# Batches half the layers apart, slab-wise keys and values, and maxima on a clock of slab lengths, in a four-layer cross-attention kernel

## The chip, the core and the metric

The kernel runs on one core of one Trainium2 chip. A core has five engines that run side by side and each take their instructions strictly in order: TensorE (PE, matmuls; its weight loads are listed apart as PEld), VectorE (DVE), ScalarE (ACT), GpSimd (POOL) and SyncE (SP), which here only issues DMA transfers. The metric is the device time of one execution in microseconds (us). The clock granted to PE varies during a run; the profile gives it as a share of full speed (PEclk).

## The reference, cut to what matters

`x` is 16 batches of 256 tokens with 128 channels, `ctx` is 16 batches of 1601 keys with 64 channels. Four layers follow each other; each is a cross-attention to `ctx` and a feed-forward part, all with residuals:

```python
x = x + L0_xattn(ln(x), ctx)   # 16 heads of 8: causal self-attention plus attention to ctx
x = x + L0_ffn(ln(x))          # 32 experts, top 4
x = x + L1_xattn(ln(x), ctx)   # 16 heads of 8
x = x + L1_ffn(ln(x))          # quantised linear, depthwise convolution, silu, quantised linear
x = x + L2_xattn(ln(x), ctx)   # 16 heads of 32: self-attention block, then attention to ctx, each with a gelu part
x = x + L2_ffn(ln(x))          # 8 experts, top 1
x = x + L3_xattn(ln(x), ctx)   # 16 heads of 8
x = x + L3_ffn(ln(x))          # 16 experts, top 2, plus a shared one
```

Every attention to `ctx` is `softmax(q k^T * scale) v` over 1601 keys in float32. Batches don't depend on each other; inside one batch everything is a chain.

## The kernel before, in words

**Slabs.** An attention to `ctx` of one batch and layer is done in 4 slabs of 4 heads (`attend`). A slab has two passes. In the first, PE forms the scores of each head `g` with the queries on the partitions (28 units of matmuls, into PSUM banks), and DVE reduces each to a maximum (`mx<-bank`). At the slab's end a short piece of work (rank `ENDS`) turns the maxima into a bfloat16 triple that sums to the negated maximum (`nm`, `nmp`, `thirds`, `shift_T`, ending in the copy `nmT` on ACT). In the second pass there are 7 steps of up to 2 key tiles each: PE forms the scores again with the keys on the partitions and adds `nmT` (`st_ops`), ACT takes the exponential (`exps`, tile `p`), PE multiplies with the values (`weigh`). `normalised` divides. Layers l0, l1, l3 have heads of 8 ("8-slabs"; their sums come with the values), l2 has heads of 32 ("32-slabs"; plain float32 keys). One batch has 12 8-slabs and 4 32-slabs; the program has 256 slabs.

**Keys, queries and their transfers.** For heads of 8, keys and queries are split into a high and a low half (`split`: tiles `hl`, the high half by ACT, the low one by DVE), and each half is spread over the partitions by DMAs issued by SP (`spread`). A set of queries (`queries8`, `parts8`) takes 16 such DMAs of 32 KB. Layer l0 makes three sets for a batch: queries for `ctx`, queries and keys for its own causal attention. The halves of queries live in 3 places (`chan_r`); a place is free when its DMAs have landed.

**Places.** Tiles get places from small classes: 7 PSUM banks, 7 places `k` (keys, their halves, and the raw context `cn`), 2 places `v`, 2 transposed contexts, 6 places `w4` (query and hidden tiles), 4 `mx`. Classes `k`, `v` and the contexts are given out in the order in which the tiles were recorded.

**Who sets the order.** Nothing is issued while the program is recorded: each operation, or a run of them, becomes a unit with a rank `(level, place)`. `emit` then plays the program against costs of its own and writes, for each engine, at each moment, the ready unit of lowest rank that finds its places; for PE it adds up to three more units on other row groups. The levels are CHAIN (layer norms, projections, feed-forward parts, self-attention of l2, keys, values; always first), ENDS, OWN (the causal attention of l0), and STEPS (maxima and steps of the slabs, last). So the slabs fill what the chains leave. The order is fixed when the program is built; on the chip the engines only wait for each other's semaphores. `emit` charges 0.07 us for a DMA issue on SP (`t = 0.07` in `emit`).

**Batches.** The main loop at the end takes batches in pairs (`LANES = 2`). Both batches of a pair are loaded together, and then for each layer the first batch's 4 slabs are followed by the second's. The chain between two layers of one batch runs beside the 4 slabs of the other. The next pair begins after l3 of this one: its loading may start earlier, when places are free.

**Ranks of slabs.** Slabs are counted with `n`. Step `j` of slab `n` has the place `n + j/7`; maximum `i` of 28 has `n - 1 + i/28 - 0.4`. All slabs count as equally long.

Of the kernel before, what the change touches and what calls it, by code (L numbers as in the profile page):

```python
# [17 lines left out]
ALU = mybir.AluOpType  # L18
# [30 lines left out]

CHAIN, ENDS, OWN, STEPS = 0, 1, 2, 3  # L50

LEAD = 0.4
NAHEAD = 2


# [396 lines left out]
def model(ctx: ExitStack, tc: tile.TileContext, d, out):  # L452
# [86 lines left out]
    def bank():  # L539
        return pb.tile([P, 512], F32, tag="bank", name=name("bank"))  # L540
# [5 lines left out]
    def mm(o, l, r, start=True, stop=True, free=False):  # L546
        nc.tensor.matmul(out=o, lhsT=l, rhs=r, start=start, stop=stop, skip_group_check=free)
# [94 lines left out]
    def new(tag, shape, base, dtype=F32, loose=False):  # L642
        return prog.tile(classes[tag], shape and list(shape), dtype, name(base), loose)
# [222 lines left out]
    def exps(att, sc, n, r):  # L866
        e = new("p", [P, 2, T], "p")
        nc.scalar.activation(e[:r, :n, :], sc[:r, :n, :], AF.Exp, scale=att.scale)
        return e

    def values8(tag, nt, z=None):


        v = new(tag, [P, nt * 144 + 24], tag)
        v9 = v[:, :-24].rearrange("p (t h e) -> p t h e", h=H, e=9)
        with prog.behind(z):
            if nt == NT:
# [113 lines left out]
    def value_tiles(x, w):  # L991

        for t0, ms in ((0, (4, 4)), (4, (3, 2))):
            ps2 = [bank(), bank()]
            with prog.together():
                for i in range(ms[0]):
                    for h in range(2):
                        if i < ms[h]:
                            r = rows_of(h * NL + t0 + i)
                            mm(ps2[h][:r, i * P : (i + 1) * P],  # L1000
                               x[h * CC : (h + 1) * CC, (t0 + i) * P : (t0 + i) * P + r], w[h * CC : (h + 1) * CC, :])
            for h in range(2):
# [7 lines left out]
    def keys(ctxT, l):  # L1010
        ks = {}
        if l == "l2":
            for s in range(4):
                t = new("k", [P, NK], "k32")
                for k0, k1, p in halves(wkv2[:, s * P : (s + 1) * P], ctxT[1], NK):
                    evac(t[:, k0:k1], p)
                ks[s] = t
        else:
            hl = [new("k", [P, NKE], "hl", F32R) for _ in range(2)]
            bias = W.get(l + "_bck")  # L1020
            for k0, k1, p in halves(W[l + "_Wck"], ctxT[0], NKE):
                split([t[:, k0:k1] for t in hl], p, bias)
            for s in range(4):
                t = new("k", [P, NKE], "k8", F32R, loose=True)
                spread(t, hl, s, True)
                ks[s] = t
        return ks

    def values(ctxT, l):
        vs = {}  # L1030
        if l == "l2":
            for s in range(4):
                v = new("v", [P, NT, P], "v32")
                for t, m, r, p in value_tiles(ctxT[1], wkv2[:, 512 + s * P : 512 + (s + 1) * P]):
                    evac(v[:r, t : t + m, :].rearrange("p t e -> p (t e)"), p)
                vs[s] = v
        else:
            v, v9 = values8("v", NT, ctxT[0])
            for t, m, r, p in value_tiles(ctxT[0], W[l + "_Wcv"]):
                evac(v9[:r, t : t + m, :, :8], p.rearrange("p (t h e) -> p t h e", t=m, h=H))  # L1040
            vs[0] = v
        return vs

    slab_no = [0]

    def attend(att):

        steps = [(t, min(2, NT - t), rows_of(t)) for t in range(0, NT, 2)]
        w = NKE if att.d8 else NK
        for s in range(4):  # L1050
            mx = new("mx", [P, 2, 4, 4], "mx", loose=True)
            stretches = [(range(q, q + 1), c * 512, c * 512 + 512) for q in range(2) for c in range(3)]
            stretches.append((range(2), 3 * 512, w))
            n = slab_no[0]
            slab_no[0] += 1
            for i, (qs, k0, k1) in enumerate(stretches):
                for g in range(4):
                    with prog.at(STEPS, n - 1 + (4 * i + g) / (4 * len(stretches)) - LEAD):
                        h = slice(32 * g, 32 * g + 32)
                        m, j = k1 - k0, k0 // 512  # L1060
                        p = bank()[:, : m * len(qs)].rearrange("p (q k) -> p q k", k=m)
                        with prog.together((g,)):
                            for q in qs:
                                mm(p[:, q - qs[0], :], att.q[h, s, q * P : (q + 1) * P], att.k[s][h, k0:k1])
                        nc.vector.tensor_reduce(mx[:, qs[0] : qs[-1] + 1, g, j], p, AX.X, ALU.max)
            with prog.at(ENDS):
                nm = new("nm", [P, 2, 4], "nm")
                nc.vector.tensor_reduce(nm, mx, AX.X, ALU.max, negate=True)
                sh = new("nmp", None, "nmp")
                thirds(sh, nm)  # L1070
                nmT = shift_T([sh])[:, 0, :]
            av = None
            for j, (t0, m, r) in enumerate(steps):
                with prog.at(STEPS, n + j / len(steps)):
                    pr = [exps(att, t, m, r) for t in st_ops(att, s, t0, m, r, nmT)]
                    if av is None:
                        av = accumulators("acc")
                    weigh(att, s, av, pr, t0, m, r, t0 + m == NT)
            with prog.at(ENDS):
                normalised(att, s, av)  # L1080
        return att.o


    def route(logits, n, k, gate):
# [277 lines left out]


    prog.recording = True
    for b0 in range(0, nb, LANES):
        lanes = range(b0, min(nb, b0 + LANES))
        ctxTs, lives = {}, {}
        for b in lanes:
            with prog.at(CHAIN):
                ctxTs[b] = load_ctx(b)  # L1370
                lives[b] = life(b, ctxTs[b])
        atts = {}
        for l in LAYERS:
            for b in lanes:
                with prog.at(CHAIN):
                    if l == "l0":
                        atts[b] = next(lives[b])
                with prog.at(CHAIN):
                    ks = keys(ctxTs[b], l)
                    vs = values(ctxTs[b], l)  # L1380
                atts[b].k, atts[b].v = ks, vs
                attend(atts[b])
                with prog.at(CHAIN):
                    atts[b] = next(lives[b], None)
    with tc.manual_schedule():
        prog.emit()

# [118 lines left out]
```

## Time and profile before

| | |
|---|---|
| median of 3 runs | 9560.31 us (9547.48 to 9571.74) |
| the profiled execution's own time | 9500.53 us |
| its span, first to last instruction | 9498.8 us |
| mean granted PE clock | 0.904 |
| PE busy | 8874.5 us (93%) |
| DVE, ACT, POOL busy | 5863.8 us (62%), 5171.3 us (54%), 1080.9 us (11%) |
| DMA issues of queries, `q<-hl` | 1024 of 32 KB, 1.9 us to landing |

How to read it: a busy PE is not a PE at full speed, because a matmul takes about twice as long while the granted clock is 0.5. So the text that follows multiplies the busy share of a stage by its granted clock and calls that the stage's useful share. The program has 8 pairs, and the same pattern comes back about every 1180 us; the second pair (from about 1140 us) is the one shown.

### The profile page before, as it was taken

The numbers are of one execution on the slowest core, as the hardware profiler recorded it, in microseconds if no ns is written. First come the engines' busy times: TensorE is split into PE (matmuls) and PEld (weight loads), VectorE is DVE, ScalarE is ACT, GpSimd is POOL, SyncE is SP. The second block draws the span as 40 slices with busy tenths as digits, with TensorE's granted clock in tenths as the row PEclk, the third lists the DMA queues.
The fourth block names the chain that finished last, engine by engine and source line by source line (L and its number), as shares of the span: only waits on it lengthen the run. The fifth ranks groups of instructions, "written<-read, shape, count | busy, mean of one in ns | idle before, by whom it ended". The sixth has DMA issues, their size and how long they took to land.

```text
span 9498.8 us, 210842 instructions
## 1 busy us (share of the span) xinstructions
PE 8874.5 (93%) x86118; PEld 5239.1 (55%) x86118; DVE 5863.8 (62%) x12308; ACT 5171.3 (54%) x10590; POOL 1080.9 (11%) x2747
## 2 busy tenths in 40 slices
PE   6999899998999989999899998999989999899999
PEld 3556555565555655556455564555645556455565
DVE  4755657556675565755667555676566755567555
ACT  2654556555564555645556454664555645566455
POOL 2011110111101011010110101101010010100100
PEclk7989889898898988989899897898988989899898
DMA  2200212002120021200212002120011101111011
GB/s 55 49 18 15 45 37 54 14 14 48 38 52 11 14 49 36 53 11 18 47 39 49 11 18 46 39 49 11 20 45 44 43 11 21 45 45 44 11 22 32
DMA packets 158879, 313.48 MB, mean 33 GB/s; under 512 B 65163, under 2 KB 116275, under 8 KB 157910
## 3 DMA queue, kind: packets, MB, share of 16 engines
q1 hardware_dynamic: 154676, 297.83, 13.6%
q8 instruction: 678, 11.11, 0.5%
q14 instruction: 291, 2.38, 0.1%
q0 software_dynamic: 768, 1.48, 0.0%
q10 hardware_dynamic: 2466, 0.68, 0.0%
HBM read 98.31 MB, written 2.10 MB: 11 GB/s over the span
## 4 chain that ended last, share of the span: by engine, by line
PE 80%; DVE 8%; ACT 4%; SPq 3%; issue 2%; DMA 2%; POOL 1%; ACTq 0%; DVEq 0%; POOLq 0%
PE bank L395 53%; PE st L395 22%; PE mx L395 4%; DVE mx L395 4%; SPq L395 3%; ACT p L395 3%; DMA k<-hl 1%; DVE z L395 1%; DVE x L395 1%; DVE st L395 1%; DMA ws<-in_s_l3f_dram 1%; DVE mv L395 0%; POOL nmp L395 0%; ACT ctxT L395 0%; DVE rc L395 0%
## 5 line engine op out<-in xcount | busy, mean ns | idle before, releaser
L395 DVE TENSOR_REDUCE mx<-bank 128x1 f32<-128x512 f32 (+2 forms) x7168 | 4093.1, 627 | 1967.6 <-PE bank L395 1871.6
L395 ACT ACTIVATE p<-st 128x512 f32<-128x512 f32 (+1 forms) x7680 | 3849.8, 575 | 2460.8 <-PE st L395 2310.6
L395 PE MATMUL st<-q,k 32*128 32x256 f32 (+1 forms) x18176 | 2531.6, 370 | 154.6 <-ACT p L395 105.7
L395 PE MATMUL bank<-k,q 32*128 32x512 f32 (+2 forms) x10240 | 2375.5, 521 | 174.8 <-DVE hl L395 88.6
L395 PEld LDWEIGHTS st<-q,k 32*128 32x128 f32 (+1 forms) x18176 | 1644.3, 190 | 1011.0 <-issue 361.7
L395 PE MATMUL bank<-p,v 128*32 128x256 f32 (+1 forms) x27648 | 2105.8, 412 | 0.0
L395 PE MATMUL st<-nmT,ones 32*128 32x512 bf16 (+1 forms) x7680 | 1682.0, 389 | 0.0
L395 PEld LDWEIGHTS bank<-k,q 32*128 32x128 f32 x10240 | 1042.2, 198 | 740.5 <-ACT p L395 199.5
L395 PEld LDWEIGHTS bank<-p,v 128*32 128x32 f32 (+1 forms) x27648 | 757.6, 114 | 896.6 <-issue 607.5
L395 POOL CAST nmp<-nm 128x8 bf16<-128x8 f32 x384 | 84.4, 220 | 4852.8 <-DVE nm L395 4465.1
L395 PE MATMUL bank<-p,ones 128*32 128x256 f32 (+1 forms) x7680 | 586.2, 384 | 0.0
L395 PEld LDWEIGHTS <-ones 32*128 32x128 bf16 (+1 forms) x7680 | 485.8, 98 | 116.5
L395 DVE TENSOR_REDUCE nm<-mx 128x2 f32<-128x512 f32 (+1 forms) x768 | 378.8, 520 | 253.8 <-PE mx L395 238.0
L395 DVE RECIPROCAL rc<-bank 128x8 f32<-128x8 f32 (+1 forms) x384 | 276.1, 719 | 293.0 <-PE bank L395 287.2
L395 POOL TENSOR_SCALAR_AFFINE_SELECT p<-p 128x512 f32<-128x512 f32 x512 | 300.3, 624 | 701.2 <-PE bank L395 490.0
L395 ACT ACT_TABLE_LOAD x222 | 284.8, 1283 | 149.5 <-PE st L395 108.0
L395 PE MATMUL mx<-k,q 32*128 32x256 f32 x1536 | 305.4, 426 | 63.0 <-DMA k<-hl 42.8
L395 POOL TENSOR_TENSOR rs<-rs,neghalf 128x2 f32<-128x2 f32 x240 | 170.3, 710 | 1663.3 <-DVE rs L395 1648.9
L395 PEld LDWEIGHTS bank<-p,ones 128*32 128x32 f32 (+1 forms) x7680 | 248.5, 111 | 178.0 <-issue 10.6
L395 ACT COPY v<-bank 128x512 f32<-128x512 f32 (+3 forms) x592 | 232.5, 451 | 144.5 <-PE bank L395 143.9
L395 PEld LDWEIGHTS mx<-k,q 32*128 32x128 f32 x1536 | 216.4, 215 | 164.5 <-issue 46.2
L395 PEld LDWEIGHTS bank<-ws,h 128*128 128x128 f32 x1664 | 231.7, 222 | 46.6 <-issue 32.3
(221 smaller groups left out, 6545.0 us busy)
## 6 DMA issues: line engine op xcount, KB each, us to landing
k<-hl SPq DMA_DIRECT2D x768, 200.2 KB, 3.6
q<-hl SPq DMA_DIRECT2D x1024, 32.0 KB, 1.9
ws<-in_s_l_a_li_dram SPq DMA_DIRECT2D x32, 768.0 KB
ws<-in_s_l3f_dram SPq DMA_DIRECT2D x32, 768.0 KB, 7.3
ws<-in_s_l0f_dram SPq DMA_DIRECT2D x32, 512.0 KB, 6.0
ws<-in_s_l_a_qkv_dram SPq DMA_DIRECT2D x16, 768.0 KB, 4.2
k<-hl SPq DMA_DIRECT2D x256, 32.0 KB, 1.9
ws<-in_s_l3f_dram SPq DMA_DIRECT2D x16, 384.0 KB
```

Of the source, the lines that this page charges most:

```text
L395: getattr(getattr(self.nc, e), method)(*a, **k)
```

## The change

- **The order of batches.** `slabs_in_order` writes one list of slabs for the whole program. After a start (l0 of batches 0 and 1, l1 of batch 0) it repeats, for each batch b: l0 of b+1, l2 of b, l1 of b+1, l3 of b (l0 of b+1 is left out for b = 0, where it has gone already). Between two layers of one batch there are always 4 or 8 slabs of another, except where the program starts and ends: l2 of batch 0 directly follows l1 of batch 0, and l3 of batch 15 directly follows l2 of batch 15. A batch is loaded alone (`begun`), recorded just before the first slab of l3 of the batch two before it.
- **Keys and values of l2** are recorded slab by slab (`keys32`, `val32`), each before its slab, and no longer four of each ahead of the layer.
- **The steps wait for the values:** each step's units, the scores and exponentials too, now depend on the writers of the values (`prog.behind`).
- **Ranks.** `clock` gives each slab a beginning on a time line in planner microseconds, 18 for an 8-slab and 34 for a 32-slab. Its steps are spread over that length. Its 28 maxima are spread over 18 us that end at least 4 us before the beginning.

```diff
-LEAD = 0.4
+LONG8, LONG32, LONGM, LEAD = 18, 34, 18, 4
...
+    def attend(att, s, begin, ahead):
...
-                    with prog.at(STEPS, n - 1 + (4 * i + g) / (4 * len(stretches)) - LEAD):
+                with prog.at(STEPS, ahead + (4 * i + g) * LONGM / (4 * len(chunks))):
...
-                with prog.at(STEPS, n + j / len(steps)):
+            with prog.at(STEPS, begin + j * (LONG8 if att.d8 else LONG32) / len(steps)), prog.behind(att.v[0 if att.d8 else s]):
...
+    def slabs_in_order():
+        def whole(b, l):
+            return [(b, l, s) for s in range(4)] if b < nb else []
+
+        seq = whole(0, "l0") + whole(1, "l0") + whole(0, "l1")
+        for b in range(nb):
+            x, y = whole(b, "l2"), whole(b + 1, "l0") if b else []
+            if y:
+                seq += y + x
+            else:
+                seq += x
+            seq += whole(b + 1, "l1") + whole(b, "l3")
+        return seq
+
+    def clock(seq):
+        begin, t = [], 0.0
+        for _, l, _ in seq:
+            begin.append(t)
+            t += LONG32 if l == "l2" else LONG8
+        ahead, t = [], 1e9
+        for t0 in reversed(begin):
+            t = min(t, t0 - LEAD) - LONGM
+            ahead.append(t)
+        return list(zip(seq, begin, reversed(ahead)))
...
-    for b0 in range(0, nb, LANES):
...
-        for l in LAYERS:
-            for b in lanes:
...
-                    ks = keys(ctxTs[b], l)
-                    vs = values(ctxTs[b], l)
-                atts[b].k, atts[b].v = ks, vs
-                attend(atts[b])
+    begun(0)
+    begun(1)
+    for (b, l, s), begin, ahead in clock(slabs_in_order()):
+        att, ctxT = atts[b], ctxTs[b]
+        with prog.at(CHAIN):
+            if l == "l2":
+                att.k[s], att.v[s] = keys32(ctxT, s), val32(ctxT, s)
+            elif s == 0:
+                att.k, att.v[0] = keys8(ctxT, l), val8(ctxT, l)
+        if l == "l3" and s == 0:
+            begun(b + 2)
+        attend(att, s, begin, ahead)
+        if s == 3:
+            with prog.at(CHAIN):
+                atts[b] = next(lives[b], None)
```

`begun(b)` loads the context and `x` of batch b and records its life up to the queries of l0. `keys8` and `val8` are the old branches for heads of 8.

More of the change, by code (lines that the diff above doesn't have):

```diff
@@ L1008, in value_tiles, with keys8 @@
                     yield t + whole, 1, r, ps2[h][:r, whole * P : m * P]
-    def keys(ctxT, l):
+    def keys8(ctxT, l):
         ks = {}
[L1012 to L1026, printed above, removed]
-        return ks
@@ L1029, in values @@
[L1029 to L1042, printed above, removed]
@@ L1044, in model, with keys32 @@
-    slab_no = [0]
-    def attend(att):
+        hl = [new("k", [P, NKE], "hl", F32R) for _ in range(2)]
+        bias = W.get(l + "_bck")
+        for k0, k1, p in halves(W[l + "_Wck"], ctxT[0], NKE):
+            split([t[:, k0:k1] for t in hl], p, bias)
+        for s in range(4):
+            t = new("k", [P, NKE], "k8", F32R, loose=True)
+            spread(t, hl, s, True)
+            ks[s] = t
+        return ks
+    def keys32(ctxT, s):
+        t = new("k", [P, NK], "k32")
+        for k0, k1, p in halves(wkv2[:, s * P : (s + 1) * P], ctxT[1], NK):
+            evac(t[:, k0:k1], p)
+        return t
@@ new lines, in val8, with val32 @@
+    def val8(ctxT, l):
+        v, v9 = values8("v", NT, ctxT[0])
+        for t, m, r, p in value_tiles(ctxT[0], W[l + "_Wcv"]):
+            evac(v9[:r, t : t + m, :, :8], p.rearrange("p (t h e) -> p t h e", t=m, h=H))
+        return v
+    def val32(ctxT, s):
+        v = new("v", [P, NT, P], "v32")
+        for t, m, r, p in value_tiles(ctxT[1], wkv2[:, 512 + s * P : 512 + (s + 1) * P]):
+            evac(v[:r, t : t + m, :].rearrange("p t e -> p (t e)"), p)
+        return v
+    def attend(att, s, begin, ahead):
@@ L1048, in attend @@
         steps = [(t, min(2, NT - t), rows_of(t)) for t in range(0, NT, 2)]
         w = NKE if att.d8 else NK
[L1050 to L1057, printed above, removed]
-                    with prog.at(STEPS, n - 1 + (4 * i + g) / (4 * len(stretches)) - LEAD):
[L1059 to L1073, printed above, removed]
-                with prog.at(STEPS, n + j / len(steps)):
[L1075 to L1080, printed above, removed]
@@ L1081, in attend @@
-        return att.o
+        chunks = [(range(q, q + 1), c * 512, c * 512 + 512) for q in range(2) for c in range(3)]
+        chunks.append((range(2), 3 * 512, w))
+        mx = new("mx", [P, 2, 4, 4], "mx", loose=True)
+        for i, (qs, k0, k1) in enumerate(chunks):
+            for g in range(4):
+                with prog.at(STEPS, ahead + (4 * i + g) * LONGM / (4 * len(chunks))):
+                    h = slice(32 * g, 32 * g + 32)
+                    m, j = k1 - k0, k0 // 512
+                    p = bank()[:, : m * len(qs)].rearrange("p (q k) -> p q k", k=m)
+                    with prog.together((g,)):
+                        for q in qs:
+                            mm(p[:, q - qs[0], :], att.q[h, s, q * P : (q + 1) * P], att.k[s][h, k0:k1])
+                    nc.vector.tensor_reduce(mx[:, qs[0] : qs[-1] + 1, g, j], p, AX.X, ALU.max)
@@ new lines, in attend @@
+        with prog.at(ENDS):
+            nm = new("nm", [P, 2, 4], "nm")
+            nc.vector.tensor_reduce(nm, mx, AX.X, ALU.max, negate=True)
+            sh = new("nmp", None, "nmp")
+            thirds(sh, nm)
+            nmT = shift_T([sh])[:, 0, :]
+        av = None
+        for j, (t0, m, r) in enumerate(steps):
+            with prog.at(STEPS, begin + j * (LONG8 if att.d8 else LONG32) / len(steps)), prog.behind(att.v[0 if att.d8 else s]):
+                pr = [exps(att, t, m, r) for t in st_ops(att, s, t0, m, r, nmT)]
+                if av is None:
+                    av = accumulators("acc")
+                weigh(att, s, av, pr, t0, m, r, t0 + m == NT)
@@ new lines, in attend @@
+        with prog.at(ENDS):
+            normalised(att, s, av)
+    def slabs_in_order():
[10 more added lines that the diff above has]
+        return seq
@@ L1364, in model, with begun @@
     prog.recording = True
-    for b0 in range(0, nb, LANES):
-        lanes = range(b0, min(nb, b0 + LANES))
-        ctxTs, lives = {}, {}
-        for b in lanes:
+    ctxTs, lives, atts = {}, {}, {}
+    def begun(b):
+        if b < nb:
             with prog.at(CHAIN):
@@ L1371, in model @@
                 lives[b] = life(b, ctxTs[b])
-        atts = {}
-        for l in LAYERS:
[L1374 to L1378, printed above, removed]
-                    ks = keys(ctxTs[b], l)
-                    vs = values(ctxTs[b], l)
-                atts[b].k, atts[b].v = ks, vs
-                attend(atts[b])
-                with prog.at(CHAIN):
-                    atts[b] = next(lives[b], None)
+                atts[b] = next(lives[b])
+    begun(0)
[13 more added lines that the diff above has]
+                atts[b] = next(lives[b], None)
     with tc.manual_schedule():
```

## The prediction

> **What bounds the kernel now.** I read the page's busy times first. PE is busy 93% of the span and DVE 62%, so only PE can bound. I then cut one pair into stages and asked for busy time and granted clock in each. The columns are window, length, busy time of PE, PEld, DVE, ACT and POOL, then PEclk.
>
> ```profile
> 1140.00:1300.00 160.00, 133.03 (x881) 76.44 (x878) 71.44 (x156) 65.26 (x137) 35.06 (x84) 0.75 0.17 44
> 1300.00:1680.00 380.00, 363.62 (x3623) 209.36 (x3626) 275.92 (x576) 248.27 (x518) 20.50 (x76) 0.92 0.22 50
> 1680.00:1920.00 240.00, 223.20 (x1822) 132.24 (x1826) 140.19 (x316) 116.60 (x233) 34.20 (x87) 0.86 0.03 11
> 1920.00:2180.00 260.00, 258.45 (x3095) 159.48 (x3087) 145.86 (x282) 129.87 (x264) 22.69 (x56) 1.00 0.09 18
> 2180.00:2314.00 134.00, 127.02 (x1350) 75.20 (x1349) 97.36 (x204) 86.06 (x175) 18.99 (x35) 0.95 0.19 40
> ...
> 1820.00:1880.00 60.00, 48.77 (x240) 26.78 (x232) 39.40 (x109) 16.51 (x33) 8.76 (x16) 0.80 0.04 14
> ```
>
> Useful share (busy share times clock): change of pair 133.03/160 x 0.75 = 0.62; l0 and l1 363.62/380 x 0.92 = 0.88; l1 to l2 223.20/240 x 0.86 = 0.80; l2 0.99; early l3 0.90. Four more pairs give 0.62 for the change of pair (0.61 to 0.62), 0.87 to 0.94 for l0 and l1, and 0.76 to 0.80 for l1 to l2. A well-covered stage of 8-slabs thus has 0.89. Two stages lie below, for different reasons.
>
> The first is the change of pair. Both new batches make their three sets of queries and keys for l0 together: 96 small DMAs that the planner charges at 0.07 us, in SP's queue:
>
> ```profile
> 1151.91 4.94 SPq L395 DMA_DIRECT2D q<-hl  x8
> 1157.03 1.12 SPq L395 DMA_DIRECT2D k<-hl  x2
> 1158.24 6.66 SPq L395 DMA_DIRECT2D q<-hl  x8
> 1165.00 1.17 SPq L395 DMA_DIRECT2D k<-hl  x2
> 1166.27 10.66 SPq L395 DMA_DIRECT2D q<-hl  x16
> 1176.98 1.06 SPq L395 DMA_DIRECT2D ws<-in_s_l3f_dram  x2
> 1178.14 11.46 SPq L395 DMA_DIRECT2D q<-hl  x16
> 1189.69 10.10 SPq L395 DMA_DIRECT2D k<-hl  x16
> 1199.89 10.34 SPq L395 DMA_DIRECT2D q<-hl  x16
> ```
>
> Sixteen issues take 10.1 to 11.5 us, some 0.65 us each. DVE must wait to write the next half, everything behind it waits too, and PE stands (a line from the timeline of PE, the idle time in brackets, and two from the waits of this stage):
>
> ```profile
> 1173.92 0.80 PE L395 MATMUL bank<-k,q 32*128 32x512 f32 x2 [12.31 <-DVE hl L395]
> ...
> DVE hl L395 <- DMA q<-hl: 16.7, 2, 12.3
> PE bank L395 <- DVE hl L395: 15.8, 2, 12.3
> ```
>
> The second is l1 to l2. The first batch's l1 ends at about 1682 us; its feed-forward part, self-attention and next queries run until 1839 us, its first maxima until 1873 us. Its cover, the other batch's l1, ends at 1828 us. Between 1820 and 1880 us the useful share is 48.77/60 x 0.80 = 0.65, and ACT waits:
>
> ```profile
> 1859.61 0.59 ACT L395 COPY hT<-bank 128x512 f32<-128x512 f32 x1 [7.98 <-PE bank L395]
> 1863.40 0.59 ACT L395 COPY hT<-bank 128x512 f32<-128x512 f32 x1 [3.20 <-PE bank L395]
> 1878.03 0.37 ACT L395 CAST nmT<-bank 128x256 bf16<-128x256 f32 x1 [14.05 <-PE bank L395]
> ```
>
> **The change part by part.** No operation is added or removed; it is an edit of order. Each stage is priced as its length times the share lost against 0.89.
>
> *l1 to l2.* Now 8 slabs of 8 heads lie under this chain (l3 of the batch before, l0 of the one after). A slab takes about 21 us (28 exponentials, 24 to 30 in 20 us), so the cover is over 170 us against a chain of 157 plus maxima of 34, much of it slowed by the very slabs that cover it. I count the hole as gone: 240 x (1 - 0.79/0.89) = 27 us in each of 8 pairs, **-216**.
>
> *The change of pair.* It disappears as a stage: 160 x (1 - 0.62/0.89) = 48.5 us at 7 places, **-340**. But the three sets stay, one batch at a time, for batches 2 to 15. What one such preparation costs isn't in the trace. Its floor is 0 (nothing waits if the 48 issues, 31 us, fit under other work); its ceiling is the price of two together, 48.5. By the number of issues it is half, 24. I take 16, by the waiting halves: with 3 places, 9 of 12 halves wait for an earlier one's DMAs in a pair, and 3 of 6 in a single batch, and waiting halves are what the PE row above ends on. 14 x 16 = **+224** (ends 0 and 679). These 48 DMAs, 5 of loading and 16 of l0's keys are moved past l3's key DMAs on SP, and POOL's 1.6 us passes over the context past its `thirds`; 85 us of l3 slabs cover both. Without that cover l0's first slab is late by SP's 31 us, and that is inside the ceiling.
>
> The change of pair has three waits of PE over 3.4 us (12.31, 3.51, 6.58 us), and after them a pair of 256-column matmuls takes 1.22 us and not 0.70. Their price is inside the 48.5, and so inside the 16.
>
> [...]
>
> *Start and end.* l2 of batch 0 now has no cover at all under its chain. The second batch's chain in the trace, with little beside it, takes 61 us to its first self-attention product, that attention 58, the rest 27, and the maxima 34: about 165 us allowing for overlap, at the hole's 0.65: 165 x (1 - 0.65/0.89) = +45. At the end l3 of batch 15 is bare: queries 52 us after l2 (2216 to 2268 us in this pair), then a slab of maxima, 21, at the share of the program's first 140 us, where only chains run (52.71/140 x 0.73 = 0.27): 73 x (1 - 0.27/0.89) = +51. l1 to l2 of batch 15 has 4 slabs only: +27. Together **+123**.
>
> *Ranks.* In a run of 8-slabs the last maximum ranked 8 us ahead of the next slab (0.4 x 20); now 4. From `nm` to `nmT` takes 2.1 us in the trace (1085.05 to 1087.16), less than 4, and ACT waits for PE's scores 2310.6 us in total, so PE is late, not this chain: **0**. A shorter lead that cost the whole 2.1 us per slab would be 256 x 2.1 = +538; a gain is bounded by the 0.11 lost in l0 and l1, of which the page lists no wait on `nmT` to win, so about -50.
>
> *Waiting for the values, slab-wise keys.* **0**: a value place comes free a whole slab (35 us in l2) before it is needed, and its copies take 2 to 3 us on ACT. Behind a waiting score stand this slab's exponentials, then DVE's maxima for lack of banks. Uncovered, it is 3 us in each of 64 slabs, +190. A gain isn't excluded (banks are not held by early scores); the PE-after-ACT waits, 105.7 us, bound it.
>
> **Sum:** -216 - 340 + 224 + 123 = -209. The profiled execution took 9500.5 us (span 9498.8 plus 1.7), so 9291; the median of the runs shown is 60 us above it, and I carry that along: **9350 us**.
>
> **Rivals.**
> - *The preparation hides.* Each costs nothing: 9350 - 224 = 9126. For it: single sets of queries for l1 (1514 to 1525 us) fall in stages at 0.88. Against: it is three sets in a row.
> - *The preparation costs a batch what it cost a pair* (slower). It now falls where l2's chain to l3 ends, whose 16 query DMAs queue behind 48 others, and l3's first slab needs them. 9350 + 14 x 32.5 = 9805. It decides from 9350 + 14 x 15 = 9560, that is from 31 us a batch. For it: SP's 10 us a set. Against: half as many issues.
> - *The chains collide on places, so nothing much moves.* Six `w4` places; l3's queries hold one, l0's three sets three, l2's self-attention four. If the two chains go one after the other, the l1-to-l2 hole stays, and l0's own sets come late: -340 + 224 + 75 of the start and end: about 9560 - 41 = 9520; with 24 us a batch it is no change.
> - *The shorter lead bites* (slower). At half of 2.1 us a slab, 256 x 1.05 = +269, 9620; it decides at 0.82 us a slab.
>
> **How the numbers follow.** Forecast 0.43, hidden preparation 0.12, dear preparation 0.17, collision 0.16, shorter lead 0.12. A measurement of this kernel can tell about 0.3%, 29 us, from no change. Faster: the forecast's 0.43 less 0.04 for its own spread (half of that no change, half slower), plus 0.12, plus 0.09 of the collision: 0.60. Same: 0.07 + 0.02 = 0.09. Slower: 0.17 + 0.12 + 0.02 = 0.31. The range must leave out at most 2 in 10: the low end is the hidden preparation, 9120; the high end takes the shorter lead and part of the dear preparation (24 to 40 us a batch), 9690. The likeliest case alone reaches from 9240 to 9460 (preparations of 8 to 24 us).
>
> **What would show it.** Right: `mx<-bank`, `p<-st` and matmul counts unchanged; `q<-hl` in runs of up to 48 at 15 or so places; no 60 us without exponentials between 300 us and the last 250; two stages of l2 per 1110 to 1150 us; mean PEclk 0.91 to 0.93, PE busy 94 to 95%; the waits "DVE hl <- DMA q<-hl", 151.6 us now, at about 100. Wrong: those waits above 200 us; PE idle ended by `nmT`; new ACT waits at each start of l3; a hole over 100 us at the start or end.

## The result, and the profile after

The changed kernel takes 9946.03 us (median of 4 runs, 9933.65 to 9995.25) against 9553.9 us for the kernel before: a ratio of 1.0417 (95% interval 1.0378 to 1.0456). It is slower by 4.2%. The forecast was 9350 us, the range 9120 to 9690.

The same maxima (7168), exponentials (7680), matmuls and query transfers (1024) are done as before. Only the loads of ACT's tables went up, from 222 to 278, which is 72 us of ACT's busy time (284.8 to 356.7, 1283 ns a load) and no explanation of the loss: the fastest variant below (e5) has 278 of them too. These are the lines of the page of the changed kernel that answer to those of before (busy times; the granted clock in 40 slices; the chain that ended last; groups of instructions with count, busy time, mean and the idle time before them):

```profile
span 9946.6 us, 210673 instructions
...
PE 9174.1 (92%) x86118; PEld 5419.8 (54%) x86118; DVE 5862.6 (59%) x12308; ACT 5228.1 (53%) x10646; POOL 1075.8 (11%) x2747
...
PEclk7988987989889898898989889799798988979898
...
PE 80%; DVE 8%; SPq 4%; ACT 3%; issue 2%; DMA 1%; POOL 1%; ACTq 0%; DVEq 0%; POOLq 0%
...
L397 PE MATMUL mx<-k,q 32*128 32x256 f32 x1536 | 337.9, 446 | 185.4 <-DMA k<-hl 185.4
```

The mean granted clock fell from 0.904 to 0.876. Two losses can be read for any run: PE's idle time (span less PE busy) and what half speed costs, span x (1 - clock), since the clock is only ever 1.0 or 0.5 in these records and a stretch at 0.5 is counted as half lost. Before: 624 and 912 us. After: 773 and 1233 us, so +148 idle and +321 at half speed, of a span that grew by 448 (the two overlap a little, since PE also idles at half clock). PE's busy time less half of what of it lies at half clock (1601 and 2170 us), that is the work at full speed, stayed the same: 8074 and 8089 us for the same 86118 matmuls. That counting half is right is an estimate from these two sums: they would agree exactly if a given work took 2.1 times as long at half clock. What single records show is less than double: `bank<-p,v` (128x256) has a median of 379 ns at full and 634 at half clock, a group of sixteen takes 1.07 and 1.94 us.

The stages show where. These are two periods of the changed kernel, in the columns of the prediction's stage table (window, length, busy times of PE, PEld, DVE, ACT, POOL, then PEclk; the last two are the DMA share and GB/s):

```profile
880.00:1000.00 120.00, 102.50 (x658) 59.93 (x659) 60.28 (x138) 44.26 (x89) 24.39 (x64) 0.73 0.17 41
1000.00:1230.00 230.00, 221.00 (x2177) 126.35 (x2178) 142.72 (x306) 145.31 (x295) 18.79 (x48) 0.93 0.11 27
1230.00:1400.00 170.00, 164.03 (x1736) 103.72 (x1729) 95.32 (x182) 77.91 (x160) 7.93 (x26) 0.90 0.13 27
1400.00:1500.00 100.00, 91.78 (x845) 50.19 (x844) 68.30 (x146) 61.63 (x128) 14.82 (x31) 0.83 0.18 37
1500.00:1620.00 120.00, 103.74 (x631) 59.96 (x632) 58.68 (x134) 43.27 (x86) 24.48 (x64) 0.71 0.16 41
...
1860.00:2020.00 160.00, 154.24 (x1688) 96.90 (x1687) 89.73 (x179) 75.53 (x156) 7.91 (x26) 0.91 0.14 29
2020.00:2120.00 100.00, 92.09 (x865) 51.67 (x864) 68.66 (x144) 62.71 (x131) 14.79 (x31) 0.85 0.20 40
```

- The preparation of one batch (880 to 1000, 1500 to 1620) is a 120 us stage of useful share 0.62 and 0.61. A pair's was 160 us at 0.62, and it now comes twice as often.
- l2 (1230 to 1400, 1860 to 2020) has 0.87 and 0.88. Before it had 0.99.
- The stage after l2 (1400 to 1500, 2020 to 2120) has 0.76 and 0.78.

SP's queue in the preparation, with the PE line that ends it (timelines of both, from the changed kernel):

```profile
1507.83 5.02 SPq L397 DMA_DIRECT2D q<-hl  x8
1512.89 0.59 SPq L397 DMA_DIRECT2D k<-hl  x1
1513.58 10.10 SPq L397 DMA_DIRECT2D q<-hl  x16
1523.77 10.09 SPq L397 DMA_DIRECT2D k<-hl  x16
...
1531.49 0.76 PE L397 MATMUL mx<-k,q 32*128 32x256 f32 x2 [11.11 <-DMA k<-hl]
```

Sixteen issues take 10.1 us; behind the third set PE stands for 11.11 us and goes on at half clock (0.5 from 1524 to 1558 us). Over the run PE waits 185.4 us in this place (16 waits, the longest 14.2). Before it was 42.8 us; these are the two waits of the kernel before that are compared below (total, times, longest):

```profile
DVE hl L395 <- DMA q<-hl: 151.6, 21, 16.1
...
PE mx L395 <- DMA k<-hl: 42.8, 6, 11.0
```

### The profile page after: what moved, and what is told of

It is laid out like the page before. It is cut to its first block, busy times and chain, and to the rows that moved or that the text cites. A ratio compares the mean times of both kernels' runs of the same rounds, so it can differ in the third digit from the quotient of the medians.

```text
span 9946.6 us, 210673 instructions
## 1 busy us (share of the span) xinstructions
PE 9174.1 (92%) x86118; PEld 5419.8 (54%) x86118; DVE 5862.6 (59%) x12308; ACT 5228.1 (53%) x10646; POOL 1075.8 (11%) x2747
## 3 DMA queue, kind: packets, MB, share of 16 engines
q10 hardware_dynamic: 2466, 0.68, 0.0%
## 4 chain that ended last, share of the span: by engine, by line
PE 80%; DVE 8%; SPq 4%; ACT 3%; issue 2%; DMA 1%; POOL 1%; ACTq 0%; DVEq 0%; POOLq 0%
PE bank L397 52%; PE st L397 23%; PE mx L397 4%; SPq L397 4%; DVE mx L397 4%; ACT p L397 3%; DMA k<-hl 1%; DVE rc L397 1%; DVE z L397 0%; DVE x L397 0%; DVE st L397 0%; DVE nm L397 0%; DVE mv L397 0%; POOL nmp L397 0%; DMA cn<-in_ctx_dram 0%
## 5 line engine op out<-in xcount | busy, mean ns | idle before, releaser
L397 PE MATMUL st<-q,k 32*128 32x256 f32 (+1 forms) x18176 | 2577.5, 379 | 186.3 <-ACT p L397 119.8
L397 PE MATMUL bank<-k,q 32*128 32x512 f32 (+2 forms) x10240 | 2260.7, 512 | 131.9 <-ACT p L397 49.0
L397 PEld LDWEIGHTS st<-q,k 32*128 32x128 f32 (+1 forms) x18176 | 1668.0, 196 | 1061.8 <-issue 346.7
L397 PE MATMUL st<-nmT,ones 32*128 32x512 bf16 (+1 forms) x7680 | 1726.9, 394 | 0.0
L397 PE MATMUL bank<-p,ones 128*32 128x256 f32 (+1 forms) x7680 | 606.4, 394 | 3.6 <-ACT p L397 3.6
L397 PE MATMUL mx<-k,q 32*128 32x256 f32 x1536 | 337.9, 446 | 185.4 <-DMA k<-hl 185.4
L397 ACT ACT_TABLE_LOAD x278 | 356.7, 1283 | 232.5 <-PE st L397 188.9
L397 PEld LDWEIGHTS mx<-k,q 32*128 32x128 f32 x1536 | 238.4, 231 | 314.3 <-issue 223.0
L397 ACT COPY y<-bank 128x256 f32<-128x256 f32 x256 | 96.2, 376 | 339.9 <-PE bank L397 323.0
```

The source lines that it names most:

```text
L397: getattr(getattr(self.nc, e), method)(*a, **k)
```

## The experiments

Three suspects stand: the clock ranks of the maxima, the preparations that come batch by batch (with the planner's charge of 0.07 us for an issue that takes 0.65), and the slab-wise keys with the wait for values. All ratios are to the kernel before, measured beside each.

**Round one: one part alone, and the charge.** `e1_ranks_alone` is the kernel before with only the ranks changed. `e2_old_ranks` is the changed kernel with the old ranks:

```diff
-with prog.at(STEPS, ahead + (4 * i + g) * LONGM / (4 * len(chunks))):
+with prog.at(STEPS, n - 1 + (4 * i + g) / (4 * len(chunks)) - 0.4):
...
-with prog.at(STEPS, begin + j * (LONG8 if att.d8 else LONG32) / len(steps)), ...
+with prog.at(STEPS, n + j / len(steps)), ...
```

`e3_sp_cost` (on the changed kernel) and `e4_before_sp_cost` (on the kernel before) alter one number of the planner, from which it works out the order:

```diff
                 if e == "sync":
-                    t = 0.07
+                    t = 0.65
```

> Order of the kernel before (pairs, keys and values a layer at a time, steps that do not wait for the values), but slabs ranked by the clock of lengths as in the changed kernel. Theory A (ranks): 18 us of maxima packed into a 34 us slab overload DVE for half a slab and leave it idle for the other, so PE waits in l2; the changed kernel's l2 stages have a useful share of 0.87 to 0.89 where the kernel before has 0.99, some 18 us a batch. Then this kernel takes 9560 + 16 x 18 = about 9850, with l2 stages at 0.90 or less. Theory B (preparations): the loss is in the single preparations of l0 (useful share 0.62 over 120 us, 36 us each), ranks are nothing: 9530 to 9590, l2 at 0.99.

> The changed kernel with the ranks of the kernel before (slabs counted, maxima 0.4 slab ahead). Theory A (ranks): l2 goes back to 0.99 and 16 x 18 = 290 us come back, about 9660. Theory B (preparations): 9900 to 9990, as the changed kernel.

> The changed kernel, but the planner charges 0.65 us for a DMA issue on SP, as measured, and not 0.07; nothing else. Theory B (preparations, by the planner's wrong price for 48 issues in a row): the engines are given other work while the halves wait; at least half of 14 x 36 = 500 us comes back, 9700 or less, and the stage of a preparation rises from 0.62 to above 0.75. Theory A (ranks): within 100 us of 9946. If the stall is the transfers themselves and not their planning, no change either.

> The kernel before, with 0.65 us charged for a DMA issue on SP. Theory B: the change of pair (48.5 us each, 7 of them, and the start) loses half or more: 9350 to 9430. If the planning of SP is not the cause of that stage's loss: 9530 to 9590.

Measured: e1 9955.59 us, 1.0453 (1.0407 to 1.0499). e2 9833.35, 1.0322 (1.0282 to 1.0362). e3 9758.45, 1.0223 (1.018 to 1.0265). e4 9417.16, 0.9885 (0.9847 to 0.9923). e4 came as theory B had it; the other three fell outside the ranges of both theories. So neither is the whole cause, and the losses don't add: the ranks alone cost as much as the whole change, and the order without the new ranks still costs 3.2%. The true charge helps both kernels, the changed one by 188 us and the one before by 114.

**Round two: the two mends together, the sets, and the third part.** `e5_old_ranks_sp_cost` has the edits of e2 and e3. `e6_no_own_sets` and `e8_before_no_own_sets` leave two of the three sets of l0 out, on the changed kernel and on the one before; the causal attention uses the queries of the attention to `ctx` in their place, so part of the computation is another one:

```diff
-qs = queries8("l0_Wq", "l0_bq", zT)
-k = parts8(new("w4", [P, 4, T], "k8", F32R, loose=True), "l0_Wk", "l0_bk", zT, True)
+qs = k = oth.q
```

`e7_slabs_alone` is the kernel before with only the third part of the change, in the place where a slab begins:

```diff
+if not att.d8:
+    with prog.at(CHAIN):
+        att.k[s], att.v[s] = keys32(ctxT, s), val32(ctxT, s)
...
-with prog.at(STEPS, n + j / len(steps)):
+with prog.at(STEPS, n + j / len(steps)), prog.behind(att.v[0 if att.d8 else s]):
```

> The changed kernel with the old ranks of maxima and steps, and with the planner charging SyncE 0.65 us instead of 0.07 us for an issue. Each alone took away 113 us (old ranks) and 188 us (charge) of the 9946 us. If they are separate causes they add: 9645 us, ratio 1.012. If both work on the same stretches (the planner's order around the preparation), the second takes away little: 9740 to 9760 us, ratio 1.022 to 1.025. Either is still slower than the kernel before with the charge alone (9417 us), since the preparation still comes 14 times instead of 7.

> The changed kernel, where the causal self-attention of l0 takes the queries of the following attention as its own queries and keys: two of the three projected sets of a batch, and 32 of the 48 small transfers that spread them over the partitions, are left out, so the output is another one. Theory (SyncE's issues and the transfers are what the preparation waits for): the folded loss around it, 44.7 us a batch, falls to 15 to 25 us, 14 times: 9530 to 9670 us. Rival (the dependent chain of normalisation, projection, softmax and evacuations is what costs): the loss stays at 35 to 45 us, 9830 to 9930 us.

> The kernel before, its order of pairs and its ranks, with the keys and values of l2 made slab by slab, and with the steps held behind their values. Theory: this part costs nothing of its own, 9490 to 9570 us, ratio 0.997 to 1.003. Rival: the values arrive late in a slab and the waits for them are part of the loss of the change: over 9620 us.

> The kernel before, where the causal self-attention of l0 takes the queries of the following attention as its own queries and keys (two of three projected sets of a batch left out, another output). Theory (issues and transfers): the folded loss of 50.0 us a pair falls to about 20 us, 7 to 8 times: 9290 to 9350 us, ratio 0.975 to 0.981, about half of what the same edit takes from the changed kernel. Rival (the dependent chain): within 60 us of 9550 us.

Measured: e5 9379.39 us, 0.9845 (0.9799 to 0.9891). e6 9722.71, 1.02 (1.0154 to 1.0247). e7 9540.86, 1.001 (0.9982 to 1.0038). e8 9304.47, 0.9776 (0.9725 to 0.9828).

e5 was a miss of my expectation (9645, or 9740 to 9760): the two mends give more together than apart. With both, the changed order is 1.6% faster than the kernel before, but most of that is the charge: against e4, which has the old order and the same charge, it is 38 us, and the intervals of the two ratios overlap. In e7 the traces show the same operations in the same order on ACT, DVE, POOL and SP as in the kernel before. So the slab-wise keys and the wait for values change nothing in the order of pairs; no run leaves them out of the half-layer order. e8 came as the theory had it; e6 fell between theory and rival. The two sets are worth 226 us in the kernel before and 223 us in the changed one, not twice as much. Taking the sets away mends half of the loss of the changed kernel; the rest is somewhere else.

What the charge does shows in the waits. First the lines of the changed kernel, then of e5 (total, times, longest):

```profile
DVE hl L397 <- DMA q<-hl: 188.3, 32, 15.9
...
PE mx L397 <- DMA k<-hl: 185.4, 16, 14.2
...
PE bank L397 <- DVE hl L397: 52.6, 18, 10.0
```

```profile
DVE hl L397 <- DMA q<-hl: 23.1, 3, 12.8
...
PE bank L397 <- DVE hl L397: 3.4, 2, 1.8
...
PE mx L397 <- DMA k<-hl: 0.5, 1, 0.5
```

With the true charge the planner counts 31 us of SP for the sets (48 x 0.65) where it counted 3.4. The charge alone mends the preparation: these are its two windows in e3 (useful shares 0.76 and 0.78), which keeps the clock ranks, and one in e2 (0.64), which keeps the old charge. In the changed kernel they were 0.62 and 0.61.

```profile
900.00:1020.00 120.00, 114.72 (x834) 67.17 (x838) 72.52 (x163) 56.40 (x113) 25.33 (x68) 0.80 0.15 35
1500.00:1620.00 120.00, 115.61 (x846) 67.02 (x846) 72.05 (x162) 56.54 (x113) 25.27 (x68) 0.81 0.15 35
```

```profile
1500.00:1620.00 120.00, 105.29 (x682) 60.18 (x684) 65.09 (x141) 43.54 (x83) 27.01 (x70) 0.73 0.14 36
```

**Round three: what in the ranks costs.** The new ranks differ from the old in two ways: in l2 the 28 maxima are packed into 18 us of a slab of 34, and the lead shrinks (0.4 of a slab was 7.2 or 13.6 us, now 4). `e9_spread_short_lead` and `e10_packed_old_lead` are e1 with one of the two each. `m` is the length of the slab ahead, and the last bracket holds the start and the length of the window of the maxima (cut from `clock`; e1 first):

```diff
-            t = min(t, t0 - LEAD) - LONGM
...
+        return [(x, t0, (t0 - LEAD - m, m)) for x, t0, m in zip(seq, begin, before)]            # e9
...
+        return [(x, t0, (t0 - 0.4 * m - LONGM, LONGM)) for x, t0, m in zip(seq, begin, before)] # e10
```

`e11_ranks_sp_cost_pairs` is e1 with the charge of 0.65, and `e12_longer_lead` is e5 with `- 0.8` in place of `- 0.4`.

> The kernel before, its order of pairs, with the new ranks split in two: here the maxima of a slab are spread evenly over a window as long as the slab ahead of it (18 or 34 us), and only the lead is the new one, 4 us in place of 7.2 or 13.6 us. All of the new ranks together made this kernel 424 us slower. Theory P (packing 28 maxima into 18 us of a slab of 34 us is what costs, since VectorE takes 28 x 0.63 = 17.6 us for them and TensorE runs at its pace): 9500 to 9620 us here. Rival L (the shorter lead makes the steps wait for their maxima): 9800 to 9960 us.

> The kernel before with the other half of the new ranks: the maxima packed into 18 us whatever the slab's length, but ending 0.4 of the slab ahead (7.2 or 13.6 us) before the steps, as in the kernel before. Theory P (packing): 9800 to 9960 us. Rival L (lead): 9500 to 9620 us. If neither alone brings it, both come out near 9530 us or both between.

> The kernel before with the new ranks and with 0.65 us charged for an issue of SyncE: the eighth corner of order (pairs or half-layer), ranks (old or clock) and charge (0.07 or 0.65). If the ranks cost the same with the right charge, as they did in the half-layer order (9758 against 9379 us, +379): 9417 + 379 to 424 = 9796 to 9841 us. If the ranks only cost because the planner's clock runs away from the chip's, the charge heals it: 9420 to 9500 us.

> The changed kernel's order and parts with the old ranks and the charge of 0.65 us (9379 us), with the maxima 0.8 of a slab ahead in place of 0.4. Rival L (a short lead costs): a longer one gains or does nothing, 9300 to 9390 us. Theory P says nothing on it but that it does not help: 9370 to 9480 us.

Measured: e9 9783.45 us, 1.0254 (1.0206 to 1.0301). e10 9713.22, 1.0192 (1.0136 to 1.0248). e11 9852.82, 1.0316 (1.0267 to 1.0364). e12 9762.85, 1.0231 (1.0186 to 1.0277). Neither half is innocent: against the 9558.2 us measured beside them the short lead costs 225 and the packing 155, together nearly the 424 of e1. Both lie between the ranges of the two theories, the third case of e10's expectation. e11 says that the true charge does not heal the ranks. e12 was a surprise outside both ranges: a longer lead costs 383 us against e5.

All eight corners of the ranks, the charge and the order of batches, in us (medians of different rounds, in which the kernel before took 9530 to 9558; the rows of the half-layer order hold the third part too):

| order of batches | ranks | charge 0.07 | charge 0.65 |
|---|---|---|---|
| pairs | old | 9531 (before) | 9417 (e4) |
| pairs | clock | 9956 (e1) | 9853 (e11) |
| half the layers apart | old | 9833 (e2) | 9379 (e5) |
| half the layers apart | clock | 9946 (the change) | 9758 (e3) |

The clock ranks cost 425 and 436 in pairs, 113 and 379 in the new order. The new order costs 302 with old ranks and the low charge, and gains 38 with the true one; with the clock ranks it gains 10, which is noise, and 94.

The two halves cost in different places. This is the l2 stage of the second pair, with some 3780 matmuls each, in the kernel before, e1, e9 and e10:

```profile
1894.00:2213.00 319.00, 316.16 (x3774) 198.60 (x3770) 180.37 (x340) 157.48 (x320) 27.85 (x77) 0.99 0.09 19
```

```profile
1948.00:2290.00 342.00, 336.04 (x3787) 208.70 (x3787) 178.75 (x342) 157.01 (x324) 27.69 (x77) 0.95 0.08 18
```

```profile
1935.00:2260.00 325.00, 322.53 (x3770) 199.32 (x3766) 179.58 (x339) 158.88 (x323) 27.72 (x77) 0.98 0.09 19
```

```profile
1921.00:2265.00 344.00, 340.93 (x3790) 212.99 (x3793) 180.10 (x343) 157.97 (x325) 27.67 (x77) 0.94 0.08 17
```

Packing lengthens it from 319 to 344 us, and the short lead only to 325. What packing does can be seen inside l2. Both kernels here have the same order and the low charge; seven windows of half a 32-slab, the maxima on DVE alone (busy, count, then PEclk, DMA share and GB/s), first of the changed kernel, then of e2:

```profile
1260.00:1277.00 17.00, 0.31 (x1) 0.96 0.07 18
1277.00:1294.00 17.00, 14.52 (x28) 1.00 0.11 23
1294.00:1311.00 17.00, 3.40 (x7) 1.00 0.19 43
1311.00:1328.00 17.00, 13.91 (x26) 1.00 0.18 31
1328.00:1345.00 17.00, 4.27 (x7) 0.55 0.09 20
1345.00:1362.00 17.00, 2.36 (x4) 0.85 0.00 1
1362.00:1379.00 17.00, 12.16 (x24) 0.85 0.26 50
```

```profile
1260.00:1277.00 17.00, 6.62 (x11) 1.00 0.26 52
1277.00:1294.00 17.00, 6.50 (x14) 1.00 0.10 25
1294.00:1311.00 17.00, 8.97 (x15) 1.00 0.26 51
1311.00:1328.00 17.00, 8.05 (x16) 1.00 0.01 2
1328.00:1345.00 17.00, 7.66 (x13) 1.00 0.27 49
1345.00:1362.00 17.00, 8.15 (x17) 1.00 0.01 2
1362.00:1379.00 17.00, 9.06 (x15) 0.95 0.26 50
```

With the old ranks 11 to 17 maxima fall in every window, and the clock holds. With the new ones 24 to 28 come together and 1 to 7 in between; in one of the thin windows the clock falls to 0.55.

I also cut every run into whole slices of 20 us, sorted them by what they hold, and summed the loss (PE idle, and half of PE's busy time at half clock). "l2" are slices with 45 or more of the sums `bank<-p,ones` that only l2 has, "mixed" have 5 to 44 of them, "8-wide" fewer but at least 15 exponentials, "few" fewer exponentials than that:

```
us lost in          l2   mixed   8-wide   few
before              39      96     475    806
e4 (charge)         33     163     492    637
e1 (ranks)          44     316     581    932
e10 (packed)        52     237     462    853
e9 (short lead)     38     183     597    897
e2 (order)          58     201     558    880
the change          62     379     497    915
e3 (change+charge)  58     401     538    670
e5 (order+charge)   62     222     447    554
```

e7 and e19, which run the order of the kernel before (see below for e19), give 42, 70, 532, 809 and 39, 116, 481, 872: differences of some 60 us in one column are noise. The packing shows as mixed slices (+141), where l2 no longer runs evenly. The short lead costs in the 8-wide stages (+122), and less clearly in the mixed slices (+87) and those with few exponentials (+91). The charge takes from the slices with few exponentials, the preparations and ends (806 to 637, 880 to 554). In the changed kernel the mixed slices alone lose 283 us more than before.

**Round four: is it the clock, and is 0.4 special?** `e14_chan5` is e5 with five places for the halves (`chan_r` 3 to 5). `e15_filler` is the changed kernel with thrown-away matmuls:

```diff
-if sums and not att.d8:
+if sums and (not att.d8 or i == n - 1):
```

`e16_lead_05`, `e17_lead_03` and `e18_lead_042` are e5 with `- 0.5`, `- 0.3` and `- 0.42`; `e19_before_lead_042` is the kernel before with `LEAD = 0.42`.

> The changed kernel's order with the old ranks and the charge of 0.65 us (9379 us), with five places instead of three for the two halves of each split set (hl), so that the next set can be projected while SyncE still spreads the last. If the places hold the preparation up (the folded loss around it is 32.3 us a batch there): 10 us a batch less, 9220 to 9300 us. If SyncE's issues themselves are the pace: 9340 to 9400 us.

> The changed kernel, where each step of the 8-wide attentions also makes one thrown-away matmul for each exponential (128x32 ones against the same exponentials, into the unused half of the accumulator): 5760 more matmuls, nothing else. What they cost at full clock, worked out from l2, whose slabs take 34 us in place of 18 with 120 such matmuls more: 0.13 us each, up to 768 us where TensorE sets the pace. Theory C (the clock falls where too little of the array is in use, and comes back only where much is): the time at half clock, 2466 us, falls to under 1700 us, and the kernel takes 9800 to 10250 us. Rival (the clock falls where TensorE stands idle, which filler in the steps does not mend): 2300 to 2700 us at half clock, 10350 to 10750 us.

> As the kernel of 9379 us (half-layer order, old ranks, charge of 0.65 us), lead of the maxima 0.5 of a slab instead of 0.4. With 0.8 it took 9763 us. If that is a slope: 9450 to 9500 us; if the cost sets in only where maxima come before the keys are there: 9340 to 9420 us.

> As the kernel of 9379 us, lead 0.3 of a slab. If the short lead costs from the first microsecond (in the order of pairs 4 us in place of 7.2 or 13.6 us cost 243 us): 9440 to 9520 us; if 0.4 lies on a plateau: 9350 to 9420 us.

> The kernel of 9379 us (half-layer order, old ranks, charge of 0.65 us) with a lead of 0.42 in place of 0.4 of a slab, 0.4 to 0.7 us. If the time is a smooth function of the lead (0.5 costs 215 us): 9400 to 9440 us. If it is the order of neighbours that decides: anywhere from 9380 to 9600 us, and over 60 us away from 9420 us is a sign of it.

> The kernel before with a lead of 0.42 in place of 0.4. Smooth: 9510 to 9570 us. Order of neighbours: 9580 to 9750 us, or under 9480 us.

Measured: e14 9458.25 us, 0.9909 (0.9878 to 0.994); e15 10403.44, 1.0896 (1.0845 to 1.0947); e16 9594.71, 1.0045 (1.0017 to 1.0073); e17 9649.43, 1.0084 (1.0047 to 1.0121); e18 9378.65, 0.9829 (0.9764 to 0.9894); e19 9557.99, 1.0015 (0.9984 to 1.0047).

- Places are not what holds the preparation up: with five of them the kernel is 79 us slower than e5, outside both ranges.
- The filler missed. PE got 10,720 more matmuls (my count of 5760 was wrong), the kernel took 457 us more, which is in the rival's range, and the time at half clock fell only from 2466 to about 2200 us (2 x span x (1 - clock), clock 0.894), between the theory's range and the rival's. So filler in the steps is no mend. Whether thin stretches drop the clock it leaves open, because the intervals with little work did not get fewer (336 against 290, last section).
- 0.3 costs 270 and 0.5 costs 215 us against e5, more than either of my cases had for them. e18 and e19 say nothing on it. There are 28 maxima in a slab and 4 to a step, so a lead of 0.4 is 11.2 maxima and one of 0.42 is 11.76: in both, the first 12 maxima of a slab rank ahead of the first step of the slab before it, and every rank stays in the same order. The traces agree: in e18 and e5, and in e19 and the kernel before, ACT, DVE, POOL and SP do the same operations in the same order. So these are the same programs measured again, and whether the time is smooth in the lead isn't shown.
- Why 0.4 is the best of the leads tried stays open, and a rival to the length of the lead stands untested. Four maxima make one stretch of keys, one for each of the four heads, and `emit` issues such units together when they are on different row groups. With 12 maxima ahead a step falls between two such stretches. With leads of 0.3, 0.5 and 0.8 it is 9, 14 and 23, and with the clock ranks in a run of 8-slabs (e1, e9, the change) it is 7: the step then falls inside a stretch. No run changes the one and keeps the other, so the 225 us of e9 are what its ranks cost, not shown to be what a shorter lead costs.

e5 and e18, one program, beat both kernels, by 1.6% and 1.7% against the kernel before. It is the change with the old ranks and one number of the planner put right; the number alone gives 1.2% (e4).

## Why the prediction was wrong

Step by step, in its own terms.

- **"Ranks: 0" failed.** It weighed only the lead, against 2.1 us of the chain from `nm` to `nmT`, and set the bounds by that. The runs: 425 us for the ranks alone (e1); in the changed order, where other losses lie beside them, 113 with the low charge (e2) and 379 with the true one (e3 against e5). It did not price at all what the other half of the edit does, 28 maxima of 0.627 us (17.6 us of DVE) packed into 18 of a slab's 34 us; that half costs 155 (e10), the other 225 (e9). The upper bound, +538, held the sum, but not for its reason: with the short lead (e9) PE's weight loads wait 8.6 us in the whole run for `nmT`. So what the new ranks cost is not this chain. For the packing it is the uneven work in l2 shown above; for the lead the mechanism stays open. The rival of the shorter lead (+269) had the size of e9, but its mechanism is this wait, which the runs don't show.
- **"A stage of l2 has 0.99" failed** for the same reason; the sum took it over unchanged. With the old ranks (e2, 1223 to 1367 us) the stage still has 0.99. 0.87 in place of 0.99 in a 170 us stage is 170 x (1 - 0.87/0.99) = 21 us in each of some 15 stages, an estimate of 310 us.
- **"Single preparations: 14 x 16 = +224" was too small.** By its own formula one costs 120 x (1 - 0.62/0.89) = 36 us, 14 x 36 = 510. The reasoning by waiting halves looked at DVE alone: those waits rose only from 151.6 to 188.3 us, between the marks given for right and wrong. The wait that grew is PE's own for the last key transfers, 42.8 to 185.4 us. The rival "a preparation costs a batch what it cost a pair" (48.5) was nearer, and it decides from 31. Its cause is the planner's charge: with that alone put right (e3) the stages have 0.76 and 0.78, which is 120 x (1 - 0.77/0.89) = 16 us, what I took; in e5 (870 to 990 and 1450 to 1570 us) they have 0.75 and 0.73, 20 us.
- **"l1 to l2: -216" did not come.** The stage after l2 now loses 100 x (1 - 0.77/0.89) = 13.5 us a batch, 27 a pair: as much as the hole that should have gone. Which chain it waits for, no run separates.
- **"The change of pair: -340" held** as far as it goes: no such stage is left.
- **"Start and end: +123" held roughly.** PE's idle time and half of its busy time at half clock sum to 1425 us before and 1858 us after. Of this a pair loses 169 us in the repeating part before, and a batch 107 after (from one loading of context to the next). Seven pairs or fourteen batches leave some 242 and 355 us for start, end and one pair: +112.
- **"Values and slab-wise keys: 0"** held in the order of pairs, 1.001 alone (e7); in the new order it isn't tested.

The three failed sums are 310 + 286 + 216 = 812 us against a miss of 657 (9948 profiled, 9291 forecast for it). They come to a quarter too much; they rest on windows drawn by hand, and their sizes are estimates.

That e5 (9379) lies within 30 us of the forecast (9350) is chance. The forecast took 209 us off a kernel with the charge of 0.07, and at that charge the order with the old ranks costs 302 (e2); of what e5 gains, the charge alone brings 114 (e4) and the order 38. From one loading of context to the next, two batches take 1177 us before, 1224 in the changed kernel, 1163 in e4 and 1147 in e5: with the charge right the order saves some 15 us in each of six pairs, and the rest of the span is 62 us longer. The profile did show where to look: the prediction read 0.65 us an issue beside a charge of 0.07, and priced the lateness in one row only, when the planner makes every order around these sets by that charge.

The forecast's sum has the half clock only inside the useful shares, and expected a mean clock of 0.91 to 0.93; it is 0.876. The runs show 321 us more at half speed, most of it beside a PE that was busy: of 640 us more at half clock, PE is busy in 569. That 3.4 us, the prediction's mark for a wait of PE, is a threshold of anything, no run shows; in its stage the next longest wait after 12.31, 6.58 and 3.51 us is 0.60.

## What to carry to other kernels

Where an order is planned ahead, check its charges against the trace before the order itself is judged: with the old ranks, one number (0.07 for 0.65 us) makes the difference between 3.2% slower and 1.6% faster. A stream that runs under a slower one (maxima under the steps of l2) is better spread evenly than bunched: bunching it made the l2 stage 344 us in place of 319. And before a trial of a parameter is read, see that it changes the program: a lead of 0.42 does not. Last, a change of three parts should be priced part by part with every part's edit read for what it moves: the ranks looked like a change of units and, made alone, cost as much as the whole change.

## What the hardware showed that I had not expected

In these records the clock falls beside a busy PE. All changes of the granted clock lie on a grid of 3.413 us. For each such interval I summed, over the matmuls at work, duration x rows/128 x columns/128 and divided by the interval: a measure of the array in use (128x128 is the largest matmul of these records; where matmuls overlap it is over 1, up to 2.0 before and 2.1 after). Before: of the 291 full-clock intervals with less than 0.85 in use 59% were followed by half clock, of the 1941 with more 0.8%. After: 66% of 290, and 1.9% of 1883. PE's busy share in an interval before a drop has a median of 0.86 (before) and 0.82 (after), so "busy" does not tell. At half clock, a PE that was busy for over 99% of an interval was followed by full clock in only 47% (before) and 41% (after) of cases, so in these records one busy interval was often not enough. All this is a correlation. The one trial to use it (e15) did not have fewer thin intervals than the changed kernel, 336 and 290, and drops after 65% of them, so it neither proves nor refutes a cause.

An issue of a small transfer on SP takes 0.63 us (sixteen in 10.1), the same for the transfers of queries and of keys.
